# Turning the last block of keys earlier, and loading W_text in four pieces, in a cross-attention kernel

## The chip, the cores and the metric

The kernel runs on one core of one Trainium2 chip. A core has a matrix engine (TensorE, in the profile PE, with its weight loads as PEld), VectorE (DVE), ScalarE (ACT), GpSimd (POOL) and SyncE (SP). In this kernel SP does nothing but issue DMA transfers. The metric is the device time of one execution in microseconds (us); less is better.

## The reference

Four batches of 2048 rows of 512 features, x, attend to 77 context rows of 384 features each. Everything is 32-bit float.

```python
text_p  = x @ W_text + b_text                     # (4, 2048, 512)
audio_p = ctx_768 @ W_audio + b_audio             # (4, 77, 512)
Q = layer_norm(text_p, g1, beta1)
K = layer_norm(audio_p, g2, beta2)
V = audio_p
alpha = softmax(Q @ K.T / sqrt(512))
H = (alpha @ V) @ W_out + b_out
out = layer_norm(H + x, g_out, beta_out)
```

W_text is 512 x 512 (1 MB), W_audio 384 x 512 (0.75 MB), the context 4 x 77 rows of 384 (0.47 MB).

## The kernel before, in words

**Two stages.** The main stage works on 64 tiles of 128 rows of x. Per tile TensorE multiplies the turned rows with a matrix `mu`, prepared beforehand, that gives scores and row norms at once (`y`, L438, and `yl`, L446), and later the softmax weights with the prepared values `vw` (`h`, L529). The order of all steps of that stage is written out by hand (a loop for the first 40 tiles, a list of steps from there on) and is fixed on each engine by `in_program_order`: every engine runs its instructions in the order in which the program issues them. The change touches none of it.

**The preparation**, in front of it, builds `mu` and `vw` from the weights and the context. The change lies here. The 308 context rows are cut in three blocks: `key_blocks` are rows 0 to 77 (block 0), 77 to 205 (block 1) and 205 to 308 (block 2; in two transfers of 96 and 7 rows), loaded to `ca0` to `ca2`. NA = 3 is the number of 128-row chunks of W_audio (`wa`), ND = NH = 4 that of W_text (`wc`), NB = 3 that of the key blocks.

- `context_turned(i)` (L249): three TensorE transposes of block i (L246) to the one PSUM bank `gain`, and a ScalarE copy to `cat[i]` (L250). Block 0 is turned apart (`first_context_turned`).
- `value_product(i, ks)` (L259): one matmul with 512 columns per chunk k of W_audio, cat[i] times wa, L264. In the trace each is two instructions. Its bank is `h` for even i and `prep` for odd i.
- `value(i)` (L269): VectorE adds `ba` (b_audio, broadcast to 128 partitions) and writes `va[i]`. `statistics(i)` and `normed(i)` then give mean, variance and the normalised keys `kn[i]`, on VectorE, with the power on GpSimd (L213).
- `centre(k)` (L606): takes the mean of every row of W_text's chunk k off it, on VectorE for k = 0 and 2 (L614 to L616), on ScalarE for k = 1 and 3 (L610 to L612).
- `turn_text(j, q)` (L618): TensorE turns a 128 x 128 square of the centred chunk q. First come all j for q = 0 and 1, then all j for q = 2 and 3, each j followed by a copy of the turned W_text to `wct[j]` (L674), by ScalarE for even and VectorE for odd j.
- After it come `gram(k)` (products of W_text with itself, L631), the turned keys and values (`key_turned`, `value_turned`), `score_weights` (L326) and `score_offsets` (L344), then the main stage.

**The order of the loads.** SP issues all loads in program order: keys 0, W_audio chunk 0, keys 1, W_audio chunks 1 and 2, keys 2 (two transfers), then W_text and b_audio (L144 to L146), the rows g1, g2 and beta2 (`vec_rows`, L150), b_text and beta1 (`rows`, L156 and L157), the first group of x in four transfers (`xq`, L178), W_out, b_out, two groups of x, g_out, beta_out and the second group `xq`. W_text's buffer `wc` is one of the two `xq` buffers.

Of the kernel before, what the change touches and what calls it, by code (L numbers as in the profile page):

```python
# [48 lines left out]
def tile_xattn(  # L49
# [18 lines left out]
    nc = tc.nc  # L68
# [3 lines left out]
    ND, NA, NH = D // P, DA // P, H // P  # L72
# [17 lines left out]
    def bank(tag, name):  # L90
        return (ps2 if tag in ("h", "y") else ps1).tile([P, 4, P], F32, tag=tag, name=name)

    def flat(t):
        return t.rearrange("p k q -> p (k q)")
# [16 lines left out]
    def load(name, shape, src):  # L111
        t = const.tile(shape, F32, name=name)
        nc.sync.dma_start(out=t, in_=src)
        return t
# [26 lines left out]

    wc = xqs.tile([P, ND, T, P], F32, tag="xq", name="wc").rearrange("p k t c -> p k (t c)")
    wcd = w_text.rearrange("(k p) h -> p k h", p=P)
    nc.sync.dma_start(out=wc[:, :2], in_=wcd[:, :2])  # L144
    ba = load("ba", [P, H], b_audio.partition_broadcast(P))
    nc.sync.dma_start(out=wc[:, 2:], in_=wcd[:, 2:])  # L146

    vec_rows = const.tile([3 * NH, P], F32, name="vec_rows")
    for i, v in enumerate((g1, g2, beta2)):
        nc.sync.dma_start(  # L150
            out=vec_rows[i * NH : (i + 1) * NH, :], in_=v.rearrange("(j p) -> j p", p=P)
# [78 lines left out]
    NB = len(key_blocks)  # L230
# [10 lines left out]
    def rows_turned(src, n, tag, name):  # L241

        m = src.shape[1] // P
        pt = bank(tag, name)[:, :m, :n]
        for k in range(m):
            nc.tensor.transpose(pt[:, k, :], src[:n, k * P : (k + 1) * P], ident[:n, :n])  # L246
        return pt

    def context_turned(i):  # L249
        nc.scalar.copy(cat[i], rows_turned(ca[i], sizes[i], "gain", f"cat_ps_{i}"))  # L250
# [8 lines left out]
    def value_product(i, ks=range(NA), pv=None):  # L259

        if pv is None:
            pv = flat(bank("prep" if i % 2 else "h", f"va_ps_{i}"))[: sizes[i]]
        for k in ks:
            nc.tensor.matmul(  # L264
                pv, lhsT=cat[i][:, k, :], rhs=wa[:, k, :], start=(k == 0), stop=(k == NA - 1)
            )
        return pv

    def value(i, pv):  # L269

        n = sizes[i]
        va[i] = prep.tile([P, H], F32, name=f"va_{i}")[:n]
        nc.vector.tensor_tensor(va[i], pv, ba[:n], ALU.add)

    def statistics(i):
        n = sizes[i]
        st = prep.tile([P, 6], F32, name=f"kst_{i}")
        nc.vector.bn_stats(st[:n], va[i])
        mvs[i] = prep.tile([P, 2], F32, name=f"kmv_{i}")
        nc.vector.bn_aggr(mvs[i][:n], st[:n])  # L280
        krs[i] = prep.tile([P, 1], F32, name=f"kr_{i}")
        nc.vector.tensor_scalar_add(krs[i][:n], mvs[i][:n, 1:2], EPS)
        rsqrt(krs[i][:n], krs[i][:n])
# [322 lines left out]
    def centre(k):  # L606
        c = slice(k, k + 1)
        if k % 2:

            nc.scalar.activation(wc[:, k, :], wc[:, k, :], AF.Identity, accum_out=nmean[:, c])  # L610
            nc.scalar.mul(nmean[:, c], nmean[:, c], -1.0 / H)
            nc.scalar.activation(wc[:, k, :], wc[:, k, :], AF.Identity, bias=nmean[:, c], scale=1.0)  # L612
        else:
            nc.vector.tensor_reduce(nmean[:, c], wc[:, k, :], AX.X, ALU.add)  # L614
            nc.vector.tensor_scalar_mul(nmean[:, c], nmean[:, c], -1.0 / H)
            nc.vector.tensor_scalar(wc[:, k, :], wc[:, k, :], nmean[:, c], None, ALU.add)  # L616
# [34 lines left out]
    pv = {0: value_product(0, [0])}  # L651
    context_turned(1)
    value_product(0, range(1, NA), pv[0])
    centre(0)
    centre(1)
    for i in range(1, NB):
        pv[i] = value_product(i, range(2))
        if i + 1 < NB:
            context_turned(i + 1)
        value_product(i, range(2, NA), pv[i])  # L660
        value(i - 1, pv[i - 1])
        if i == 1:
            statistics(0)
# [80 lines left out]
    def keep_warm_late(count):  # L744
# [6 lines left out]
        k=keep_warm_late,  # L751
# [10 lines left out]
        i=invert,  # L762
# [112 lines left out]
```

## Time and profile before

| | |
|---|---|
| time, median of 3 runs | 294.86 us (294.74 to 295.93) |
| the profiled execution's own time | 295.57 us |
| its span, first to last instruction | 293.8 us |
| mean granted TensorE clock | 0.991 |
| TensorE busy | 284.0 us, 97% of the span |
| VectorE, ScalarE, GpSimd busy | 227.0, 154.4, 157.3 us |
| W_text's two transfers, issue to landing | 6.0 and 8.5 us |
| the preparation's last matmul group (`uw_ps`, L344) starts | 36.94 us |

The page of the profile gives busy times, a chain of work that ended last, and groups of instructions. The timeline of an engine lists its instructions by start, length and, in brackets, the idle time before and who ended it. The landings of transfers are those at which the trace counts their last completion; a transfer is spread over up to 16 DMA engines, and each counts its own share. Times are in us from the span's start.

### The profile page before, as it was taken

What the parts mean: (1) busy time and instruction counts of PE and PEld (TensorE: products, weight loads), DVE (VectorE), ACT (ScalarE), POOL (GpSimd) and SP (SyncE); (2) the same over time, 40 slices, a digit from 0 to 9 for tenths busy, and PEclk for the clock granted to TensorE, in tenths of its full rate; (3) what the DMA queues carried; (4) which work ended last, traced back from release to release, by engine and by line L of the source; (5) the groups of instructions that cost most, each with busy time, mean ns of one, the idle gap of its engine ahead of it and who ended that gap; (6) DMA issues with size and microseconds to landing.
All of it is one profiled execution on the core that took longest, in us unless ns stands there. A gap on an engine that the chain in (4) does not pass through costs nothing.

```text
span 293.8 us, 3988 instructions
## 1 busy us (share of the span) xinstructions
PE 284.0 (97%) x1021; PEld 168.3 (57%) x1021; DVE 227.0 (77%) x713; ACT 154.4 (53%) x490; POOL 157.3 (54%) x168
## 2 busy tenths in 40 slices
PE   8899999999999999999999999999999999999990
PEld 5385755565555555555556565656565555555540
DVE  0684243387878797979797979798999999989995
ACT  3475210041346474747373737357967767477571
POOL 1012000010116667676767676777988968977833
PEclk9999999999999999999999999999999999999996
DMA  6999933559391786979696969699789987612214
GB/s 208 249 277 345 180 94 71 86 166 197 117 250 55 155 273 144 285 151 282 145 285 148 281 148 283 144 285 177 290 168 298 211 253 201 161 71 87 110 57 178
DMA packets 54282, 55.58 MB, mean 189 GB/s; under 512 B 2585, under 2 KB 35673, under 8 KB 54259
## 3 DMA queue, kind: packets, MB, share of 16 engines
q1 hardware_dynamic: 54259, 55.33, 71.3%
q8 instruction: 8, 0.13, 0.2%
q14 instruction: 15, 0.12, 0.1%
HBM read 38.23 MB, written 16.78 MB: 187 GB/s over the span
## 4 chain that ended last, share of the span: by engine, by line
PE 91%; DVE 3%; DMA 2%; issue 1%; SPq 1%; ACT 1%; DVEq 0%
PE y L438 53%; PE h L529 18%; PE yl L446 5%; PE vw_ps L368 4%; PE m_ps L326 3%; PE et_ps L521 2%; PE w_ps_yl L631 2%; DMA wc<-in_L_xattn_W_text_dram 2%; PE va_ps L264 1%; PE w_ps_y L631 1%; DVE z L581 1%; PE uw_ps L344 1%; DVE z L542 1%; DVE y L579 1%; SPq L126 1%
## 5 line engine op out<-in xcount | busy, mean ns | idle before, releaser
L438 PE MATMUL y<-mu,xt 128*128 128x464 f32 (+2 forms) x512 | 179.6, 473 | 0.0
L438 PEld LDWEIGHTS y<-mu,xt 128*128 128x128 f32 x512 | 89.8, 191 | 49.5 <-issue 32.3
L529 PE MATMUL h<-vw,et 77*128 77x512 f32 x128 | 64.1, 594 | 0.1
L550 ACT ACTIVATE sqj<-z,sz 128x512 f32<-128x512 f32 x64 | 46.0, 719 | 31.9 <-DVE z L542 31.0
L599 POOL TENSOR_TENSOR z<-z,go 128x512 f32<-128x512 f32 x44 | 55.9, 1270 | 10.0 <-ACT z L595 9.4
L600 POOL TENSOR_TENSOR z<-z,beo 128x512 f32<-128x512 f32 x44 | 55.8, 1269 | 3.5
L542 DVE SCALAR_TENSOR_TENSOR z<-h,inv,x 128x512 f32<-128x512 f32 x64 | 46.4, 732 | 2.3 <-PE h L529 1.8
L389 DVE STREAM_TRANSPOSE xt<-xq 128x512 f32<-128x512 f32 x64 | 44.7, 703 | 0.5 <-PE y L438 0.5
L462 DVE CUSTOM_DVE_ANT_1 yl<-yl,x,bc 128x128 f32<-128x128 f32 x64 | 22.6, 353 | 28.3 <-PE yl L446 28.1
L462 DVE CUSTOM_DVE_ANT_1 y<-y,x,e 128x384 f32<-128x384 f32 x64 | 40.1, 626 | 2.3
L492 POOL TENSOR_SCALAR rs<-ss 128x4 f32<-128x4 f32 (+2 forms) x21 | 4.7, 223 | 67.8 <-DVE ss L462 67.5
L446 PEld LDWEIGHTS yl<-ub,xt 128*128 128x128 f32 x128 | 23.6, 189 | 26.2 <-issue 15.6
L595 ACT ACTIVATE z<-z,no,ro 128x512 f32<-128x512 f32 x44 | 34.5, 802 | 0.1
L522 ACT COPY et<-et_ps 77x256 f32<-77x256 f32 (+1 forms) x33 | 11.9, 361 | 39.5 <-PE et_ps L521 39.5
L213 POOL TENSOR_TENSOR ro<-ro,mhalf 128x4 f32<-128x4 f32 (+2 forms) x21 | 18.2, 868 | 23.9 <-ACT ro L562 23.8
L509 ACT ACTIVATE e<-e,mx 128x77 f32<-128x77 f32 x64 | 22.2, 349 | 11.9 <-DVE mx L502 11.9
L529 PEld LDWEIGHTS h<-vw,et 77*128 77x128 f32 x128 | 23.3, 191 | 7.0 <-issue 5.2
L446 PE MATMUL yl<-ub,xt 128*128 128x128 f32 x128 | 24.5, 273 | 0.0
L213 POOL TENSOR_TENSOR rs<-rs,mhalf 128x4 f32<-128x4 f32 (+2 forms) x21 | 18.6, 886 | 1.8
L484 DVE TENSOR_TENSOR e<-y,uws 128x80 f32<-128x80 f32 x64 | 14.9, 233 | 4.7 <-PE y L438 3.4
L521 PEld LDWEIGHTS et_ps<-ident,e 128*77 128x77 f32 x64 | 9.4, 147 | 15.1 <-issue 10.9
L579 DVE SCALAR_TENSOR_TENSOR y<-z,nm,gain_ps 128x512 f32<-128x512 f32 x20 | 14.9, 752 | 0.8
(112 smaller groups left out, 253.6 us busy)
## 6 DMA issues: line engine op xcount, KB each, us to landing
xq<-in_x_dram SPq DMA_DIRECT2D x64, 256.0 KB, 5.3
x<-in_x_dram SPq DMA_DIRECT2D x16, 1024.0 KB, 7.2
out_dram<-z SPq DMA_DIRECT2D x64, 256.0 KB, 2.1
wc<-in_L_xattn_W_text_dram SPq DMA_DIRECT2D x2, 512.0 KB, 7.2
wo<-in_L_xattn_W_out_dram SPq DMA_DIRECT2D x1, 1024.0 KB
wa<-in_L_xattn_W_audio_dram SPq DMA_DIRECT2D x3, 256.0 KB, 2.8
ba<-in_L_xattn_b_audio_dram SPq DMA_DIRECT2D x1, 256.0 KB
bo<-in_L_xattn_b_out_dram SPq DMA_DIRECT2D x1, 256.0 KB
```

What stands on the lines that cost most here:

```text
L213: nc.gpsimd.tensor_tensor(dst, v, mhalf[: v.shape[0], : v.shape[1]], ALU.pow)
L389: nc.vector.transpose(xt.rearrange("p k (a j) -> p a k j", j=R), xq[i][:, t].rearrange("p a (k i) -> p a k i", i=R),)
L438: nc.tensor.matmul(parts(y[:, : Q * AQ])[:, :, cols], lhsT=xt[:, k, :], rhs=mub[:, k, :, cols], start=(k == LAST_K), stop=(k == 0),)
L446: nc.tensor.matmul(b, lhsT=xt[:, k, :], rhs=ub.rearrange("p q i -> p (q i)"), start=True, stop=True)
L462: nc.vector.tensor_tensor_reduce(out=y, in0=y, in1=x, scale=1.0, scalar=first, op0=ALU.mult, op1=ALU.add, accum_out=to)
L509: nc.scalar.activation(e, e, AF.Exp, bias=s.mx[:, c], accum_out=s.inv[:, c])
L529: nc.tensor.matmul(s.h[n], lhsT=s.et[:, n - s.tiles[0], :], rhs=s.vw, start=True, stop=True)
L542: nc.vector.scalar_tensor_tensor(z, s.h.pop(n), s.inv[:, c], xs[i][:, t, :], ALU.mult, ALU.add, accum_out=s.sz[:, c])
L550: nc.scalar.activation(junk, s.z[n], AF.Square, bias=s.sz[:, c], scale=-float(H), accum_out=s.sq[:, c])
L595: nc.scalar.activation(z, z, AF.Identity, bias=s.no[:, c], scale=s.ro[:, c])
L599: nc.gpsimd.tensor_tensor(z, z, go, ALU.mult)
L600: nc.gpsimd.tensor_tensor(z, z, beo, ALU.add)
```

## The change

W_text's two transfers of two chunks become four of one chunk each; b_audio stays in between, behind the second. The turning of key block 2 moves from the middle of block 1's products to a place before the centring of W_text's chunks 0 and 1 and before all of block 1's products, and those products are issued in one piece. On TensorE the order was: block 0's products, block 1's chunks 0 and 1, transposes of block 2, block 1's chunk 2, block 2's products. It becomes: block 0's products, transposes of block 2, block 1's products, block 2's products. On ScalarE the copy of `cat[2]` stood behind `centre(1)` and now stands in front of it. VectorE's order stays.

```diff
     wcd = w_text.rearrange("(k p) h -> p k h", p=P)
-    nc.sync.dma_start(out=wc[:, :2], in_=wcd[:, :2])
+    for k in range(2):
+        nc.sync.dma_start(out=wc[:, k], in_=wcd[:, k])
     ba = load("ba", [P, H], b_audio.partition_broadcast(P))
-    nc.sync.dma_start(out=wc[:, 2:], in_=wcd[:, 2:])
+    for k in range(2, ND):
+        nc.sync.dma_start(out=wc[:, k], in_=wcd[:, k])
...
     pv = {0: value_product(0, [0])}
     context_turned(1)
     value_product(0, range(1, NA), pv[0])
+    for i in range(2, NB):
+        context_turned(i)
     centre(0)
     centre(1)
     for i in range(1, NB):
-        pv[i] = value_product(i, range(2))
-        if i + 1 < NB:
-            context_turned(i + 1)
-        value_product(i, range(2, NA), pv[i])
+        pv[i] = value_product(i)
         value(i - 1, pv[i - 1])
         if i == 1:
             statistics(0)
```

## The prediction, made before the changed kernel was run

> **What bounds the kernel now.** I read the page first: busy shares, then the chain that ended last.
>
> ```profile
> PE 284.0 (97%) x1021; PEld 168.3 (57%) x1021; DVE 227.0 (77%) x713; ACT 154.4 (53%) x490; POOL 157.3 (54%) x168
> ...
> PE 91%; DVE 3%; DMA 2%; issue 1%; SPq 1%; ACT 1%; DVEq 0%
> ```
>
> TensorE is the bound of nearly the whole span, so only time in which it really stands is to be had, and both edits lie in the first 15 us. TensorE's own waits (view of waits, that engine, first 42 us) are two:
>
> ```profile
> PE w_ps_yl L209 <- DVE zeros L194: 1.0, 1, 1.0
> PE va_ps L264 <- ACT cat L250: 0.9, 1, 0.9
> ```
>
> The first is the launch. The second, 0.93 us, is the hole that the reordering aims at; the chain in order of time, narrowed to 3 to 23 us, shows where it comes from:
>
> ```profile
> 3.87 5.96 DMA wc<-in_L_xattn_W_text_dram
> ...
> 10.85 0.72 ACT wc L612
> 11.58 0.31 ACT cat L250
> 11.89 0.04 issue
> 11.93 2.82 PE va_ps L264 x6
> 14.75 0.44 PE w_ps_y L620 x4
> ```
>
> W_text's first half lands at 9.84, ScalarE centres row block 1 from 9.86 (`centre(1)`, L610 to L612), and only then copies the turned last key block (`cat` L250), which stands behind it in ScalarE's program order. TensorE has finished block 1's products at 11.00 and waits for that copy until 11.93. What ScalarE and VectorE do next (timeline, each engine):
>
> ```profile
> 13.37 0.63 ACT L610 ACTIVATE wc<-wc 128x512 f32<-128x512 f32 x1 [1.49 <-DMA wc<-in_L_xattn_W_text_dram]
> 14.36 0.72 ACT L612 ACTIVATE wc<-wc,nmean 128x512 f32<-128x512 f32 x1
> ...
> 11.17 0.68 DVE L273 TENSOR_TENSOR va<-va_ps,ba 77x512 f32<-77x512 f32 x1
> ```
>
> The second half of W_text lands at 13.35, so `centre(3)` ends at 14.36 + 0.72 = 15.08. TensorE turns W_text from 14.59; the second eight transposes (blocks 2 and 3) begin at 15.46. So they were ready only 0.4 us before they were used: that is what is late next.
>
> **The change part by part.** The sum is made against the profiled execution: 295.57 us, span 293.8 and 1.8 around it. It lies 0.7 above the median of 294.86, so I carry the difference over to the median.
>
> *Block 2 turned earlier.* Its three transposes now follow block 0's products. They need the `ca` rows, whose last completion in the trace's landing records is 7.62; TensorE gets there at about 8.08 (block 1's four matmuls before the old place fill 8.08 to 9.8 at 0.44 each). No wait, 0.46 us of cover. They need the `gain` bank, free since the copy of block 1 ended at 6.56. The transposes cost what they cost before, some 0.3 us, so they only move. ScalarE is idle from 6.56 to 9.86 and does the 0.40 us copy at about 8.5. Then six half-matmuls of block 1 end at 8.4 + 6 x 0.44 = 11.0 and six of block 2 at 13.65, against 14.59 before: 0.93 earlier, the whole hole. The first eight W_text transposes (8 x 0.109) end at 14.5.
>
> *W_text in pieces.* The bytes and their order in the queue are unchanged, b_audio included: it came behind 512 KB and still does. Piece 0 lands earlier. The slowest DMA engine needed 2.93 us from the last W_audio piece (6.91) to W_text's first half (9.84) for about 23 rows of 2 KB, 0.127 each, and piece 1 is eight of them: piece 0 lands at about 8.8. VectorE's `centre(0)` (9.86 to 11.26 before) is then over by 10.3, and VectorE is free when b_audio lands (10.69 in the landing records). `value(0)` starts at 10.7 instead of 11.17: 0.45 earlier. From there to the end of `normed(2)` at 21.4 VectorE's timeline has no hole, and three times TensorE waits for it there: `gram(0)`, 1.17 us where 8 x 0.109 would do, for the last `wct` copy; keys 1 for `kn` (`normed(1)`); keys 2 likewise. So 0.45 is what VectorE's chain lets through. Its next inputs hold: block 1's products are done at 11.0, piece 2 is needed at 13.0 and lands near 12.0 (half-way between b_audio at 10.69 and 13.35).
>
> *Piece 3*, the last, decides the rest. ScalarE's `centre(3)` takes 15.08 - 13.35 = 1.73 from its landing. If it lands at 13.35 as now, TensorE's first transpose of block 3 goes from 15.57 to some 15.25, 0.32 earlier, and ScalarE's and VectorE's copies of `wct` find 0.19 of slack there (the first result for VectorE was ready at 16.06, used at 16.25). So 0.45 still passes.
>
> *Its landing* the trace does not show, so I bound it. SP issues two more transfers at 0.43 to 0.46 each. The landing records count on eight semaphores taken in turn, and SP waits for the transfer eight issues back:
>
> ```profile
> SPq L178 <- DMA wc<-in_L_xattn_W_text_dram: 2.8, 2, 2.3
> ...
> SPq L150 <- DMA wa<-in_L_xattn_W_audio_dram: 1.0, 2, 0.5
> ```
>
> That is the first x load held until W_text's first half has landed. In the new list piece 3 is the twelfth issue and waits for the fourth, W_audio's second piece (6.15): issued at 6.19 instead of 4.83, 1.36 later. Upper bound: if landing follows issue, 14.71. Lower bound: if the stretch from b_audio to piece 3 ran at the speed of the one before it (256 KB in 10.69 - 9.84 = 0.85), 10.69 + 1.70 = 12.39. I take 13.4, no change: g1, g2 and beta2 issued at 5.3, 6.2 and 6.9 landed at 13.6, 13.9 and 14.2, so the queue, not the issue, sets the landing, and at 6.6 the engines still have over 3 us of work ahead.
>
> A rule speaks against the split. The Trainium skill (DMA: Bandwidth & Descriptors, Anatomy of one DMA, and Rules for kernel authors) gives each transfer a fixed cost of about 2 us beside its bytes and asks to coalesce. Two more in series would be 4 us: piece 3 at 17.4, and a total near 298.5 as an estimate. But the rows here show 256 KB pieces of W_audio landing 0.76 apart (6.15, 6.91): the fixed part is overlapped when they queue. I go by the row.
>
> *What is pushed back.* vec_rows is issued about as before (each waits for W_audio's last piece and the keys, 6.9 to 7.6), landing near 14.2, wanted at 16.4. b_text and beta1 now wait for W_text's first two pieces: about 1 us later, landing 14.8 becomes 16, wanted by VectorE at 19.1. The first x loads wait for b_audio and pieces 2 and 3: up to 2 us, first `turn` at 29.2. From w_out on each transfer again waits for the same one as before. All of it hidden; if that cover were gone, VectorE's chain would move one for one.
>
> Sum: -0.45 by VectorE, and 0.05 given back for two more completion writes per DMA engine: -0.4 us, 295.57 to 295.2, or 294.86 to **294.5**. From 22 us on TensorE is the bound and passes the shift on.
>
> **The rivals.**
>
> *The late piece and the clock (slower).* Between the two halves TensorE now stands from 14.5 until piece 3 is centred: 0.6 us, plus every tenth that it is late. Each tenth beyond 0.3 is lost one for one. And the granted clock could fall. In stretches of 3.41 us that end where it changes (columns: stretch, PE, PEld, DVE, ACT, POOL busy, clock, DMA share, GB/s):
>
> ```profile
> 8.58:11.99 3.41, 2.48 (x9) 0.88 (x8) 2.02 (x5) 1.95 (x5) 0.00 (x0) 1.00 0.95 297
> ...
> 15.40:18.82 3.42, 3.42 (x33) 3.06 (x31) 3.35 (x10) 1.93 (x5) 0.78 (x1) 1.00 1.13 200
> ...
> 285.05:288.47 3.42, 1.49 (x5) 0.42 (x4) 3.41 (x8) 2.30 (x9) 3.32 (x4) 1.00 0.21 77
> 288.47:293.80 5.33, 0.00 (x0) 0.00 (x0) 2.30 (x4) 0.27 (x1) 0.91 (x2) 0.50 0.53 197
> ```
>
> A stretch with 2.48 busy kept the clock, one with 1.49 lost it. So with 0.6 of standing it is safe; with 1.9 (piece 3 late by 1.3, just the upper bound) it is not, and a stretch at half clock costs about 1.7. Together 1.0 + 1.7 = 2.7: 297.6. It decides from about 1.3 us of lateness. For it: the issue is later by 1.36. Against: the queue argument. The skill (TensorE: Matmul & The Clock Gate, Part 4: PE-mode transpose) would make it likelier: it says transposes do not count as busy time for the clock. After the change no ordinary matmul runs from 13.65 to about 16.5, so by the rule the clock could fall with piece 3 on time: +1.7 - 0.4, 296.2. The rows disagree: 15.40 to 18.82 had only 1.17 of ordinary matmuls (`gram(0)`), the rest transposes, and kept the clock; 285.05 to 288.47 had 1.13 and lost it. Transposes count here. Chance of slower by over 0.5%: 0.13.
>
> *Nothing comes through.* Piece 3 or b_audio is late by 0.3 to 1.0, the hole only moves from 11.0 to 14.5: 294.6 to 295.6. Chance 0.20.
>
> *More than the hole.* Holding back b_text, beta1 and x relieves the slow DMA engines (14 of 16 had finished W_text's second half by 11.75, the last two at 12.66 and 13.35). Piece 3 by 12.4 and b_audio by 10.3 would give TensorE the 0.93 and VectorE 0.85: 294.0. For over 0.5% other waits up to 22 us must go too (TensorE's work from 14.59 to 22.47 is 7.0 of 7.9 us): at most 1.8, 293.1. Chance of that 0.09.
>
> **How the numbers follow.** 0.5%, 1.5 us, is about what a measurement of this kernel can tell from no change. Forecast 0.58 (own range 294.0 to 294.8); nothing, 0.20; both are within 0.5%: 0.78 together. Slower 0.13, faster 0.09. The range leaves out about a tenth on each side: 293.9 (the whole hole) to 296.0 (into the late piece).
>
> **What would show it.** Right: `cat` of block 2 copied before 9, no TensorE wait for it, products done near 13.7, `value(0)` near 10.7, a new wait for `centre(3)` of about 0.6 at 14.5, `gram(2)` at about 21.9 instead of 22.3. Wrong: W_text's last centring starting after 13.7, a `ca` wait near 8, a granted clock under 1.00 before 288, or VectorE waiting for b_audio past 11.2.

## The result, and the profile after

The changed kernel takes 294.62 us (median of 22 runs, 294.12 to 295.26), the kernel before, run beside it, 295.25 (22 runs): a ratio of 0.9979, 95% interval 0.9971 to 0.9988, or 0.6 us less. The forecast was 294.5, within 0.5% of before; so it came. The profiled execution's own time is 294.76 and its span 293.0, 0.8 under the span of before.

The page of the changed kernel, busy times and chain by engine:

```profile
PE 283.7 (97%) x1021; PEld 168.1 (57%) x1021; DVE 227.1 (78%) x713; ACT 154.5 (53%) x490; POOL 157.6 (54%) x168
...
PE 92%; DVE 3%; DMA 2%; issue 1%; SPq 1%; DVEq 0%; ACT 0%
```

The engines do the same work; what is gone is standing. TensorE's own waits in the first 42 us, changed kernel:

```profile
PE w_ps_yl L211 <- DVE zeros L196: 1.0, 1, 1.0
PE va_ps L266 <- DMA wa<-in_L_xattn_W_audio_dram: 0.5, 1, 0.5
```

The wait of 0.9 for the copy of `cat` is no longer there; a wait for W_audio, which is issued ahead of all that the edits touch, is; the second trace of this kernel (`after_again`, below) does not have it. The chain in order of time (start, length, what):

```profile
2.54 5.10 DMA wa<-in_L_xattn_W_audio_dram
...
7.68 1.08 PE va_ps L266 x2
8.77 0.27 PE cat_ps L248 x3
9.04 5.17 PE va_ps L266 x12
14.21 0.44 PE w_ps_y L622 x4
...
27.80 8.61 PE m_ps L328 x32
```

W_text and ScalarE have left the chain: it now starts at W_audio's last piece (landed at 7.64) and runs on TensorE alone up to the score weights (`m_ps`, made by `score_weights`), block 2's transposes (8.77) in front of the twelve half-products in one piece. ScalarE and VectorE in the timeline (the number in brackets is the idle time before):

```profile
9.07 0.42 ACT L252 COPY cat<-cat_ps 128x309 f32<-128x309 f32 x1 [2.56 <-PE cat_ps L248]
...
12.20 0.63 ACT L612 ACTIVATE wc<-wc 128x512 f32<-128x512 f32 x1 [0.77 <-DMA wc<-in_L_xattn_W_text_dram]
```

```profile
9.06 0.69 DVE L616 TENSOR_REDUCE nmean<-wc 128x1 f32<-128x512 f32 x1 [5.12 <-DMA wc<-in_L_xattn_W_text_dram]
...
10.46 0.69 DVE L275 TENSOR_TENSOR va<-va_ps,ba 77x512 f32<-77x512 f32 x1
```

In the kernel before, ScalarE's copy and VectorE's `centre(0)`:

```profile
11.48 0.40 ACT L250 COPY cat<-cat_ps 128x309 f32<-128x309 f32 x1
```

```profile
9.86 0.69 DVE L614 TENSOR_REDUCE nmean<-wc 128x1 f32<-128x512 f32 x1 [5.92 <-DMA wc<-in_L_xattn_W_text_dram]
```

The copy is done at 9.5 instead of 11.88, `centre(0)` starts at 9.06 instead of 9.86, `value(0)` at 10.46 instead of 11.17, and `centre(3)` at 12.20 instead of 13.37.

One trace of these kernels carries luck of half a microsecond to a whole one in its first landings, and several profiled executions below are not at their kernel's median. So I take mechanisms from the traces and sizes from the medians. What ties them is that everything after the preparation is rigid: in the eleven traces whose clock stayed up, before and after included, the span less the start of `score_weights` (`m_ps`) is 265.1 to 265.3. In the chain of the kernel before that start is:

```profile
28.49 8.62 PE m_ps L326 x32
```

### The profile page after: what moved, and what is told of

It is laid out like the page before. It is cut to its first block, busy times and chain, and to the rows that moved or that the text cites. A ratio compares the mean times of both kernels' runs of the same rounds, so it can differ in the third digit from the quotient of the medians.

```text
span 293.0 us, 3988 instructions
## 1 busy us (share of the span) xinstructions
PE 283.7 (97%) x1021; PEld 168.1 (57%) x1021; DVE 227.1 (78%) x713; ACT 154.5 (53%) x490; POOL 157.6 (54%) x168
## 4 chain that ended last, share of the span: by engine, by line
PE 92%; DVE 3%; DMA 2%; issue 1%; SPq 1%; DVEq 0%; ACT 0%
PE y L440 53%; PE h L531 18%; PE yl L448 5%; PE vw_ps L370 4%; PE m_ps L328 3%; PE et_ps L523 2%; PE va_ps L266 2%; PE w_ps_yl L633 2%; DMA wa<-in_L_xattn_W_audio_dram 2%; PE w_ps_y L633 1%; DVE z L583 1%; PE uw_ps L346 1%; DVE z L544 1%; DVE y L581 1%; PE kt_ps L248 0%
```

## The experiments

My theory was the prediction's: two chains run side by side, TensorE's (with the hole behind ScalarE's copy) and VectorE's (from `centre(0)` on W_text's first landing through `value(0)` to the keys), and both have to move.

**Each edit alone, and both kernels again.** `order_only` is the changed kernel with W_text in halves:

```diff
-    for k in range(2):
-        nc.sync.dma_start(out=wc[:, k], in_=wcd[:, k])
+    nc.sync.dma_start(out=wc[:, :2], in_=wcd[:, :2])
     ba = load("ba", [P, H], b_audio.partition_broadcast(P))
-    for k in range(2, ND):
-        nc.sync.dma_start(out=wc[:, k], in_=wcd[:, k])
+    nc.sync.dma_start(out=wc[:, 2:], in_=wcd[:, 2:])
```

> Only the turning of key block 2 is moved; W_text stays in two transfers. My theory (two chains in parallel: TensorE's hole, and VectorE's chain that starts with centre(0) on W_text's first landing): TensorE's wait for the copy of block 2 goes, its products end near 13.7 instead of 14.6, but VectorE's value(0) stays near 11.2 and holds gram(0) and the key transposes where they were, so ratio 0.999 to 1.000. Rival A (the hole alone is the gain): ratio 0.998, as with both edits, the span shorter by 0.7. Rival B (the gain is the landing of the pieces): ratio 1.000.

Measured: 0.9998 (0.9984 to 1.0012). TensorE's waits, first 42 us, and its timeline where it stands:

```profile
PE w_ps_y L620 <- DVE wc L616: 0.4, 1, 0.4
```

```profile
15.16 0.80 PE L620 MATMUL w_ps_y<-ident,wc 128*128 128x128 f32 x4 [0.45 <-DVE wc L616]
```

The hole behind the copy is gone, and TensorE starts the W_text transposes early, only to stand in the middle of them for `centre(2)`, which VectorE reaches late because `value(0)` still starts at 11.41. Rival A, the hole alone, is out; Rival B, that the gain is the landing of the pieces, has its figure.

`pieces_only` is the kernel before with W_text in the four transfers of the change, and the old order of the turning.

> Only W_text is cut in four; the turning of key block 2 stays in the middle of block 1's products. My theory: value(0) starts near 10.5, but the copy of block 2 still stands behind centre(1) on ScalarE, which ends at landing of piece 1 plus 1.7, so the hole stays at 0.8 to 1.0 us and the ratio is 0.999 to 1.000. Rival A (the hole alone): ratio 1.000 and every part of the span unchanged. Rival B (the landings, with the DMA engines finishing evenly): ratio 0.998, as with both edits.

Measured: 0.9982 (0.9971 to 0.9992), a larger gain than I expected, and again the figure of Rival B. Its TensorE wait, ScalarE's copy, and VectorE:

```profile
PE va_ps L266 <- ACT cat L252: 1.2, 1, 1.2
```

```profile
11.72 0.40 ACT L252 COPY cat<-cat_ps 128x309 f32<-128x309 f32 x1
```

```profile
10.86 0.69 DVE L275 TENSOR_TENSOR va<-va_ps,ba 77x512 f32<-77x512 f32 x1 [1.06 <-DMA ba<-in_L_xattn_b_audio_dram]
```

The hole stays, as expected: TensorE waits 1.2 for the copy behind `centre(1)`, and here it is TensorE's chain that ends last. But I had let piece 1 land when the first half had landed. In this trace it did (10.1), and its execution was the longest of the twelve (295.55, median 294.79). In the two traces of the changed kernel it landed at 9.70 and 8.70, against 9.84 and 10.32 for the first half in the two of before. If piece 1 is early in most executions of `pieces_only` too, ScalarE's copy is as well, and that would explain the median; but this is argued from another kernel's traces and not shown.

`before_again` and `after_again` are the two kernels unchanged.

> The kernel before, unchanged, for a second trace of the same kernel and as a measure of what these rounds can tell: ratio 1.000 within 0.001. In the first trace of it two of the 16 DMA engines finished every transfer 1 to 2 us after the others; in the trace of the changed kernel none did. If that belongs to the two large transfers of W_text, it is here again (W_text's second half lands at 13 to 13.5, 14 of its 16 shares by 11.8). If it belongs to the execution, it may be absent here, and the second half then lands near 12.2.

> The changed kernel, unchanged, for a second trace: ratio 0.998. If the late DMA engines belong to the execution and not to the kernel, they may appear here, with piece 3 landing near 13.3; the span is then still 0.4 us under that of the kernel before, by the sum of the prediction. If the split removes them, piece 3 lands near 12.2 again.

Measured: 1.0002 (0.9988 to 1.0015) and 0.9982 (0.9971 to 0.9992). So the rounds can tell a little more than a part in a thousand, and the gain repeats. Against it, the median of `pieces_only` (294.79) is 0.12 above that of `after_again` (294.67), with intervals that overlap: **what the reordering adds to the pieces is not shown by the times**; that it adds nothing without them is. My theory that both chains have to move is therefore not borne out by the times. Of the late DMA engines: in `before_again` the shares of W_text's second half come in spread from 10.0 to 13.53, without two clear stragglers; in `after_again` piece 3 is complete at 11.68.

The traces of the kernels in which the clock stayed up and neither W_text's last piece nor `vec_rows` was made late, in us (the last column is what the chain in order of time runs through between `value(0)` and the score weights):

| kernel | centre(0) | value(0) | m_ps | m_ps less value(0) | chain |
|---|---|---|---|---|---|
| before | 9.86 | 11.17 | 28.49 | 17.32 | ScalarE's copy, TensorE |
| before_again | 10.35 | 11.66 | 28.97 | 17.31 | ScalarE's copy, TensorE |
| order_only | 10.09 | 11.41 | 28.72 | 17.31 | VectorE |
| halves_two_small | 10.14 | 11.45 | 28.76 | 17.31 | VectorE |
| pieces_only | 8.40 | 10.86 | 28.58 | 17.72 | ScalarE's copy, TensorE |
| after | 9.06 | 10.46 | 27.80 | 17.34 | TensorE |
| after_again | 8.06 | 9.82 | 27.19 | 17.37 | TensorE |
| fill | 8.17 | 11.14 | 28.46 | 17.32 | VectorE |
| fill_dve | 8.79 | 10.30 | 27.27 | 16.97 | VectorE |
| best | 8.61 | 10.25 | 27.00 | 16.75 | TensorE |

The last two columns are the finding. Where VectorE's order is that of before and its chain ends last, 17.31 or 17.32 us lie between `value(0)` and the score weights (`order_only`, `halves_two_small`, `fill`): VectorE's chain is a floor under the preparation, however early TensorE is. In the kernel before, TensorE's chain with the hole ends within 0.01 of that floor. In the two traces of the changed kernel TensorE's chain ends last, 0.03 and 0.06 above it. So the two chains end almost together before and after the change; `order_only` moves TensorE's alone, and VectorE's holds it on the floor. In the one trace of `pieces_only`, where VectorE starts earlier and the hole stays, TensorE's chain ends 0.4 above the floor. Except in `best`, `value(0)` starts when the first W_text transfer is centred or b_audio is there, whichever is later.

**Size or competition.** In the first six traces W_text's last transfer was complete at 13.4 to 13.6 in halves and at 11.7 to 12.6 in pieces. `halves_two_small` puts halves into the changed kernel, with two small loads behind them:

```diff
-    for k in range(2, ND):
-        nc.sync.dma_start(out=wc[:, k], in_=wcd[:, k])
+    nc.sync.dma_start(out=wc[:, 2:], in_=wcd[:, 2:])
+    for i in range(2):
+        load(f"stand_in{i}", [NH, P], g1.rearrange("(j p) -> j p", p=P))
```

(the first pair as in `order_only`).

> The changed kernel, but W_text in two transfers again, followed by two 2 KB loads of g1 that nothing reads: the same number of issues ahead of vec_rows as with four pieces, so that b_text, beta1 and the first x loads are held back as long. In the three traces with halves W_text was complete at 13.4, 13.6 and 13.5, in the three with pieces at 12.2, 12.6 and 11.7. Theory M1 (the size of the transfers makes the last DMA engine late): complete at 13.4 or later, ratio 0.999 to 1.001. Theory M2 (what follows takes the engines' time, and holding it back frees them): complete near 12.3; the first half still lands as one, so VectorE starts at about 9.8 and the ratio is 0.999 to 1.000.

Measured: 1.0001 (0.9985 to 1.0017); second half complete at 12.27, first half at 10.11. VectorE's waits:

```profile
DVE nmean L616 <- DMA wc<-in_L_xattn_W_text_dram: 6.2, 1, 6.2
```

The second half came as early as piece 3 did, and the kernel gained nothing: it is the first landing that counts. By the landing, this speaks for competition (M2).

`pieces_vec_late` is the changed kernel with the three loads of `vec_rows` behind `spread_x(0)`.

> The changed kernel, but the three vec_rows loads stand behind the first x loads, so that b_text and beta1 wait for W_audio's last piece and the keys (issued near 7.7 to 8.5) and the first x loads for the keys and pieces 0, 1 (from 8.5): nothing is held back, more competes with pieces 2 and 3 than in the kernel before. M1 (size): piece 3 lands near 12.2 all the same. M2 (competition): near 13.5. vec_rows may come after 16 and then hold the small transpose L678, so the time says less than the landing: ratio 0.998 to 1.002.

Measured: 1.0082 (1.0056 to 1.0108), from the five shorter of six executions; piece 3 complete at 12.46 with nothing held back, which speaks for size (M1), against the run above. With one trace of each, and landings that move by half a microsecond or more between executions of one kernel, **why the last piece lands earlier stays open**; that it does not matter for the time is what `halves_two_small` shows. The loss here is another one. Its profiled execution, 301.64, is the longest (the others 296.48 to 298.55), and TensorE's wait in it is:

```profile
PE vec_ps L678 <- DMA vec_rows<-in_L_xattn_beta_dram: 4.2, 1, 4.2
```

The three 2 KB loads landed at 19.9, behind a megabyte of x.

**What bounds the changed kernel.** `fill` gives TensorE two products while W_audio's last piece is on its way:

```diff
-    value_product(0, range(1, NA), pv[0])
+    value_product(0, [1], pv[0])
+    pv[1] = value_product(1, range(2))
+    value_product(0, [2], pv[0])
...
-        pv[i] = value_product(i)
+        pv[i] = value_product(i, [2], pv[1]) if i == 1 else value_product(i)
```

> The changed kernel with block 1's first two products in front of block 0's last one, so that TensorE has work while W_audio's last piece is on its way. My theory is that VectorE's chain from value(0) to the start of gram(2) (11.3 us in five traces of six) bounds the changed kernel together with TensorE: TensorE is done with the products 0.5 to 0.8 earlier, but gram(0) and the key transposes wait for VectorE, and the ratio to the kernel before is that of the changed kernel, 0.998, within 0.0005. Rival (TensorE alone bounds it, from W_audio's last landing on): 0.996.

Measured: 0.9981 (0.9969 to 0.9993), the changed kernel's ratio. Its profiled execution is the longest of twelve, with b_audio late (`value(0)` at 11.14). TensorE's earlier work is lost again at `gram(0)`, whose eight matmuls (0.87 of work) wait for VectorE's copy of `wct`, as its chain shows; the second line is the changed kernel's `gram(0)`:

```profile
16.41 1.64 PE L633 MATMUL w_ps_y<-wct 128*128 128x128 f32 x8
```

```profile
16.37 1.10 PE L633 MATMUL w_ps_y<-wct 128*128 128x128 f32 x8
```

```profile
16.31 0.61 DVE wct L677
16.92 0.04 issue
16.96 1.09 PE w_ps_y L633 x6
```

`fill_dve` shortens VectorE's chain as well: `normed(1)` in front of `value(2)`, the operations on `bmean` behind `normed(2)`, `rows_turned` behind `gram(2)`.

> As the one before, and VectorE's chain is shortened where TensorE waits for it: normed(1) in front of value(2), the three operations on b_text (1.3 us) behind normed(2), and the turning of those rows behind gram(2). If VectorE's chain is the bound, now both chains are shorter: 0.996, the products of W_text with itself (gram(2)) near 21.0 to 21.3 instead of 21.8. If TensorE's work from W_audio's last landing is the bound, the VectorE part adds nothing over the one before.

Measured: 0.9974 (0.9963 to 0.9984), a smaller gain than the 0.996 I expected, in an interval that overlaps that of `fill`. In the table 17.0 us stand instead of 17.3; `gram(0)` still took 1.64.

`best` moves on from there, and takes one of those steps back: the operations on `bmean` (the second `...`) are in front of `normed(2)` again.

```diff
-    normed(0)                      # in front of the second eight transposes of W_text
...
+    normed(0)                      # behind the copies of wct
     normed(1)
     value(2, pv[2])
     statistics(2)
     value_turned(0, "prep")
     gram(0)
-    key_turned(0, "gain")
     value_turned(1, "prep")
+    gram(1)
+    key_turned(0, "gain")
     key_turned(1, "h")
-    normed(2)
...
-    gram(1)
+    normed(2)
     value_turned(2, "prep")
+    gram(2)
     key_turned(2, "gain")
 
-    gram(2)
```

> The kernel fill_dve with two more moves: the products of W_text with itself for columns 0 and 1 directly behind its transposes and the turned keys behind them, normed(0) behind the copies of the turned W_text, the last block of keys behind gram(2). VectorE then has 1.7 us more before TensorE wants the keys. In fill_dve gram(0) took 1.64 us for 0.87 of work; if VectorE's chain was what held it, that goes to 0.9 to 1.0 and the ratio to 0.995 to 0.996. If TensorE's work from the landings on is the bound: 0.997 as fill_dve.

Measured: 0.9967 (0.9954 to 0.9980), 294.12 against 294.92. TensorE's timeline:

```profile
15.85 1.10 PE L633 MATMUL w_ps_y<-wct 128*128 128x128 f32 x8
```

`gram(0)` takes 1.10 instead of the 1.64 of `fill_dve`, which is what it took in the changed kernel, and the table's interval is 16.75. TensorE is busy in all of the 22.50 us from 4.40 to 26.90 (21.89 of them in the first trace of the changed kernel). So in this trace TensorE's own work is the bound; that is the rival's case, and the measured ratio is the rival's 0.997, though the interval holds my 0.996 too. All nine runs (293.55 to 294.40) lie below all fifteen of the kernel before (294.59 and up). That it beats the changed kernel is not shown: the intervals of the two ratios overlap, and the two were not run side by side.

**What a late piece costs, and the clock.** `late_a` issues W_text's piece 3 behind the first of the four x loads, `late_b` behind the second:

```diff
-    for k in range(2, ND):
-        nc.sync.dma_start(out=wc[:, k], in_=wcd[:, k])
+    nc.sync.dma_start(out=wc[:, 2], in_=wcd[:, 2])
...
             for q in range(Q):
+                if i == 0 and q == 1:          # 2 in late_b
+                    nc.sync.dma_start(out=wc[:, 3], in_=wcd[:, 3])
```

> The changed kernel with W_text's piece 3 issued behind the first of the four x loads. In the trace of the changed kernel centre(3) was done at 13.91 and its product first wanted at 14.95, so 1.05 us of lateness are free. Piece 3 should land near 15.0 instead of 12.2: TensorE stands about 1.8 us in the middle of the W_text transposes and the time is that much longer than the changed kernel's, 296.4, ratio 1.0045. The granted clock: by the first prediction a hole of 1.9 us in a stretch of 3.4 can cost it, so some executions may lose 1.7 to 3.4 us more. Rival (other work hides the lateness): 0.998.

> The same with piece 3 behind the second x load: landing near 16.1, TensorE stands about 2.9 us, ratio 1.008 if the clock is kept. If transposes did not count as work for the clock, it would fall in nearly every execution of this kernel and of the one before (1.7 to 3.4 us more, 1.014 to 1.020); if they do count, it falls only where the hole covers most of a stretch.

Measured: 1.0057 (1.0035 to 1.0079) and 1.0142 (1.0106 to 1.0177). Piece 3 landed at 14.51 and 15.70. TensorE's waits, `late_a` first, then `late_b`:

```profile
PE w_ps_y L623 <- ACT wc L615: 1.5, 1, 1.5
```

```profile
PE w_ps_y L623 <- ACT wc L615: 2.5, 1, 2.5
```

About one microsecond of lateness is free, as the changed kernel's trace had it, and from there TensorE stands: `late_a`'s piece is 2.3 later than in that trace, TensorE waits 1.5, and the profiled execution (296.09) is 1.3 longer. The medians lose more than the waits say, and `late_b` pays most, as the granted clock shows (columns as in the prediction), in stretches of 3.41 us cut where it changes (in `late_a` on the same grid from its first rise); `late_a` first:

```profile
15.17:18.58 3.41, 2.28 (x20) 2.09 (x21) 1.69 (x4) 2.51 (x6) 0.10 (x1) 1.00 1.15 239
```

```profile
13.55:16.96 3.41, 1.41 (x10) 0.91 (x8) 1.28 (x4) 1.17 (x4) 0.78 (x1) 1.00 1.17 212
16.96:20.38 3.42, 2.89 (x14) 2.53 (x15) 1.79 (x4) 1.83 (x4) 0.00 (x0) 0.50 1.05 334
20.38:23.79 3.41, 3.41 (x20) 3.41 (x19) 3.27 (x9) 1.52 (x6) 0.55 (x1) 0.50 1.05 387
```

A stretch with 2.28 us of TensorE kept the clock, although only 0.88 of it were ordinary matmuls (the kernel before lost it with 1.13 of them, from 285.05); one with 1.41 in all lost it, for two stretches. The four executions of `late_b` show it too: 298.01 at a mean clock of 0.989, 300.89 at 0.981. In `late_a` four of five stayed at 0.989 to 0.991. So in these stretches transposes counted for keeping the clock.

`one_transfer` loads W_text in one transfer ahead of b_audio:

```diff
-    for k in range(2):
-        nc.sync.dma_start(out=wc[:, k], in_=wcd[:, k])
+    nc.sync.dma_start(out=wc, in_=wcd)
     ba = load("ba", [P, H], b_audio.partition_broadcast(P))
-    for k in range(2, ND):
-        nc.sync.dma_start(out=wc[:, k], in_=wcd[:, k])
```

> The changed kernel with W_text in a single 1 MB transfer ahead of b_audio. By the rule that transfers be coalesced it should be no slower than four pieces: 0.998. My theory: both centre(0) and centre(1) wait for the whole megabyte, near 12, VectorE's chain starts 3 us later than with pieces and the time is about 2.5 us longer, 297.2, ratio 1.007.

Measured: 1.0121 (1.0080 to 1.0163). VectorE's first step, and the clock:

```profile
12.86 0.69 DVE L613 TENSOR_REDUCE nmean<-wc 128x1 f32<-128x512 f32 x1 [8.91 <-DMA wc<-in_L_xattn_W_text_dram]
```

```profile
16.12:19.53 3.41, 1.61 (x14) 1.42 (x15) 3.27 (x9) 1.12 (x3) 1.12 (x2) 1.00 1.14 199
19.53:22.95 3.42, 3.42 (x18) 3.19 (x18) 3.35 (x9) 1.20 (x4) 0.42 (x2) 0.50 1.04 374
```

The whole megabyte is there at 12.83, before W_text's second half in the two traces of before (13.35 and 13.53) and within 1.2 us of piece 3 in all traces that load the pieces in a row (11.68 to 12.66); but `centre(0)` waits for all of it. I had left out the clock: its loss over one stretch, 3.4 us at half speed, is 1.7 us as an estimate, about the 1.5 that the ratio exceeds my figure by. The one execution of four whose mean clock stayed at 0.992 took 296.85, near my 297.2.

## Why the prediction was right, point by point

- **VectorE's chain as the limit of the gain** was the right step: the reordering without it gives nothing (0.9998), TensorE's work moved forward gives nothing more (`fill`), and the interval from `value(0)` falls below 17.31 only where VectorE's order is changed. But it is not the only limit: in the two traces of the changed kernel TensorE's chain ends later, by 0.03 and 0.06.
- **That the hole has to close** for the pieces to pay was part of the sum, and the times do not show it: `pieces_only`, with the hole, gained 0.37 (294.79 against 295.16), not measurably less than both edits.
- **Its size, -0.45, was too small.** The term was `value(0)` at 10.7, held by b_audio at 10.69. It measured 10.46: b_audio landed at 10.36, and `centre(0)`, on piece 0 at 9.04 (8.8 forecast), ended at 10.46 and was what held it. So 0.71, in the one pair of traces, while the span fell by 0.82. By the medians the gain is 0.63, against the 0.4 forecast.
- **That the forecast time missed by only 0.1** is in part luck: it started from 294.86, the median of three runs, where 22 runs give 295.25, and the gain was 0.2 larger than forecast.
- **The hole and the turning of block 2**: the hole went, without a wait for `ca`. The products end at 14.2 and not 13.65, and the copy started at 9.07, not before 9: W_audio's last piece landed at 7.64 instead of 6.91, and TensorE's chain in that trace hangs on it. The kernel before shows that scatter too (6.91 and 7.42 in its two traces), so I take it for scatter.
- **Piece 3 unchanged at 13.4** was wrong. It landed at 12.18 and 11.68, below my lower bound of 12.39. So the forecast stand of 0.6 for `centre(3)`, one of the signs of being right, never came. It did no harm to the sum, since the sum had that stand hidden behind VectorE. Why the piece was early stays open. It and b_audio came about as early as the rival *More than the hole* asked for (12.4 and 10.3), and the time did not: 294.62, not 294.0.
- **The small change given back**, 0.05 for two more completion writes, cannot be seen.
- **The coalescing rule**: the row was the better guide. The four pieces land 0.66, 1.48 and 1.00 apart in the first trace (b_audio lies between the second and the third), not 2 us each, and the one large transfer costs 1.2% (1.0121). The section of the Trainium skill that the prediction cites for the 2 us (DMA: Bandwidth & Descriptors, Anatomy of one DMA) has that figure for transfers issued from GpSimd, and these are issued by SP.
- **The slower rival** had its mechanism right and its condition unfilled. A late piece does cost time beyond its slack, and then the clock (`late_a`, `late_b`); but the piece was early, in the split as well as with nothing held back. Its issue 1.6 us later (6.46 against 4.83), on the semaphore of W_audio's second piece, cost nothing.
- **The clock's limit**, put between 1.49 and 2.48 of 3.41, holds and is narrower now: 1.61 fell, 2.28 stayed.

## What to carry to other kernels

Before a hole on the busiest engine is closed, ask which other chain ends at the same place: here closing the hole of 0.93 us was worth nothing alone, since VectorE's chain beside it ended at the same place, and nothing measurable on top of the pieces. A transfer should be cut where its first part starts a chain; the work that follows the first part decides, not the transfer's mean speed. And where the landings move by half a microsecond or more between executions, the interval between two events of one trace says more than the time of either.

## What the runs showed of the hardware that I had not expected

- Landings scatter between executions of one kernel: W_text's first half at 9.84 and 10.32 in the two traces of before, piece 0 just before `centre(0)` started on it, at 9.06 and 8.06, and W_audio's last piece at 7.64 and 6.93 in the two of the changed kernel. The late share of two DMA engines in the first trace was not the kernel's property.
- Holding the clock and regaining it may differ. In `late_a` 2.28 us of TensorE in a stretch, mostly transposes, kept the clock at 1.00; in `late_b` 2.89, nearly all transposes, from 16.96 to 20.38 left it at 0.50 for one more. That it is the transposes that fail to bring it back is not shown, since in `pieces_vec_late` 3.06 did no better, and 2.00 of it were ordinary matmuls:

```profile
19.65:23.07 3.42, 3.06 (x18) 3.06 (x19) 2.71 (x7) 0.42 (x1) 0.47 (x1) 0.50 1.05 386
```

The Trainium skill (TensorE: Matmul & The Clock Gate, Part 4: PE-mode transpose) says that transposes do not engage the full clock; `late_a` speaks against that for holding it. What exactly brings it back these runs don't settle.
